# Moving a residual addition from GpSimd to VectorE, with three changes of order, in a fused attention and Mamba kernel

## The chip, the cores and the metric

The kernel runs on one core of one Trainium2 chip. The metric is the device time of one execution in microseconds (us); of several runs the median is given. TensorE is called PE in the profile, VectorE DVE, ScalarE ACT, GpSimd POOL, and SyncE SP; SP here only issues DMAs. "PEld" is the loading of weights into PE.

## The reference, cut to what matters

```python
# x: (8, 512, 48, 48) fp32, that is 8 samples of 512 channels by 2304 tokens
x = x + linear_causal_attention(groupnorm(x))   # 8 heads of 64; q, k = elu + 1; out = num / den
y = groupnorm(x)
prev = None
for i in range(4):                              # four slices of 128 channels
    x_i = y[i] + prev if prev is not None else y[i]
    x_m = mamba_i(x_i)                          # in_proj, conv of 4 taps, silu, x_proj, softplus,
                                                # scan over tokens with 16 states of 256 channels,
                                                # gate by silu(z), out_proj
    f = maximum(x_i, x_m)
    prev = feats[i] = sigmoid(mean(x_i)) * x_i + sigmoid(mean(f)) * f
x = x + concatenate(feats)
```

Everything is fp32.

## The kernel before, in words

Both layers run at once. The work of a sample and a slice of 128 channels is a block, 32 in all, and a block is six chunks of `LC` = 384 tokens. Two streams take the blocks by turns: stream 0 has the even samples, stream 1 the odd ones. The kernel is written out by hand in program order (a manual schedule); each engine works through its own instructions in that order, and waits are made for the data and buffers they need.

**Mamba's scan** is the frame. A chunk of a block is a `Job` (192 in all), and a job is eight slots (`SLOTS`), one for each of two halves of the 256 channels and four quarters of the 16 states. In a slot (`slot`):

- `product` on DVE (L890) and `last_product` on POOL (L879) multiply B with delta times x. POOL does the last `TAIL` columns of each of four groups, DVE the others. DVE reads B from a copy in PSUM (`Bp`), which ACT makes in `inputs` (L863).
- `decay` on ACT (L900) makes exp(A delta) in a PSUM bank, up to three ahead (`DEPTH`), five ahead in two places.
- `scan` on DVE (L910), four of them, each giving its bank back.
- `weigh` on POOL (L923) multiplies by C; `gather` on PE (L937) sums over the states into `yp`.

At the end of each half of a job DVE multiplies by the gate (`gated`, L949), and after the second PE projects (`Job.project`, L955) and DVE takes the maximum (`maximum`, L966). Tiles `u` of a slot go round in five buffers.

**All else is done beside the slots**, in stages. A slot has two halves; `beside` is called in each half, at the slot's start for the even one, behind the second scan for the odd one. Stages are Python generators wrapped in `Task`. At each yield a stage says when it is due (a half number, or a gap since its last step) and how many PSUM banks it needs (six are shared with the decays; `take` gives the first free one). `tasks` holds the Mamba stages and `heads` the attention's chunks (`chunk`). `beside` first steps the heads that need no bank, and then goes through tasks and heads in this order, so what a task issues in a half stands ahead of a head's stages that need banks:

```python
for t in heads:
    if t.need is not None and t.need[1] == 0 and t.fits() and t.due():
        t.step()
held = False
for t in tasks + heads:
```

The parts of these stages that the change touches:

- `chunk`, counted in halves from the chunk's own start (`at(j)`); chunks follow each other by 16 halves, the length of a job. At 0, 2 and 4 PE projects q, k and v (`project`, L300) and ACT and DVE make the features (L312, L313, L359, L367); L373 and L375 are the running sum of k, which ACT copies (L382) and DVE multiplies with q (L386). At 14 and 15 the denominators' reciprocals (`rd`, L433, L434) are spread over 64 columns by ACT (`rdb`, L441). At 17 PE transposes them into a bank (L445, three transposes; one bank needed). At 18 DVE multiplies q by them (L450). At 19 PE makes the masked scores in two banks (L457, L467), at 20 ACT takes their relu out (`sm`, L479) and gives the banks back, and at 22 PE reads the relus (L498). ACT copies the result (L508), and DVE takes its statistics at 28 (L512).
- `pass_on`, run at the end of each block for each of the next block's chunks c. `first` is the half at which that chunk's job begins. At first - 33 three loads go to SP's queue (`loads`: `xb`, `fu`, `xo`; L620, L623, L625), at first - 25 PE mixes two products in a bank (L678), in the next half ACT copies the mixture to `fu` (L682) and PE adds a third (L684), and in the one after that ACT makes the next block's input (L689) and POOL adds `fu` to the residual `xo` (L696). `save` puts the store to `out` on a list; `flush` issues it two halves later.
- `prepare`, for each job: the convolution on PE (L722) from first - 21, four Silus on ACT at first - 18 (L758 to L763), Softplus some halves later (L793). Exp, Silu and Softplus each need ACT's table loaded anew. `dx` is made on POOL (L834); B, C, `dr` and `dxr` are read by DMA (L812, L819, L825).
- `statistics` takes the first group norm's statistics of later samples piece by piece (L253), and `group_norm` its small arithmetic (L190 to L211).
- In the first of a sample's four attention passes POOL also normalises the input, four instructions a chunk (L324).

Of the kernel before, what the change touches and what calls it, by code (L numbers as in the profile page):

```python
# [12 lines left out]
ALU = mybir.AluOpType  # L13
# [6 lines left out]
LC = 384  # L20
NI, NQ, NGR = 4, 4, 4
SLOTS = 8
TAIL = 152
BANKS = 6
DEPTH = 3
LEAD = 11
# [23 lines left out]
def attention_then_mamba_kernel(  # L50
# [12 lines left out]
    nc = tc.nc  # L63
# [106 lines left out]
    def save(out, in_):  # L170
        stores.append((half_no[0], out, in_))

    def flush(every=True):
        while stores and (every or stores[0][0] <= half_no[0] - 2):
            _, o, i = stores.pop(0)
            nc.sync.dma_start(out=o, in_=i)
# [103 lines left out]
    def chunk(m):  # L280
# [10 lines left out]
        def at(j, gap=1):  # L291
            return times[m] + j, gap
# [146 lines left out]
        yield at(15), 0  # L439
        rdb = new("rdb", 1, (P, 2 * NT, 64))  # L440
        nc.scalar.copy(rdb, rd.unsqueeze(2).to_broadcast([P, 2 * NT, 64]))  # L441
        yield at(17), 1
        rb = bank()[:, 0:LC].rearrange("p (i t) -> p i t", i=NT)
        for i in range(NT):
            nc.tensor.transpose(  # L445
# [19 lines left out]
        for i in range(NT):  # L465
            for h, sc in zip(heads_of, scs):
# [5 lines left out]
                    stop=i == NT - 1,  # L472
                    skip_group_check=True,
                )
        yield at(20), 0
        sms = []
        for par, sc in enumerate(scs):
            sm = new(f"sm{par}", 1, (P, NT, T))
# [43 lines left out]
    class Stream:  # L522
# [55 lines left out]
        def pass_on(self):  # L578
# [9 lines left out]
            last = old is not None and old[1] == 3 and not self.samples  # L588
# [26 lines left out]
            def loads(c):  # L615
                fu = xb = xa = None
                cols = slice(c * LC, (c + 1) * LC)
                if not last:
                    xb = mpool.tile([P, LC], F32, tag="xb", name=f"xb_{self.n}_{c}")
                    nc.sync.dma_start(out=xb, in_=x1s[self.b][s * P : (s + 1) * P, cols])  # L620
                if old is not None:
                    fu = mpool.tile([P, LC], F32, tag="fu", name=f"fu_{old[2]}_{c}")
                    nc.sync.dma_start(out=fu, in_=old[3][:, cols])  # L623
                    xa = mpool.tile([P, LC], F32, tag="xo", name=f"xo_{old[2]}_{c}")
                    nc.sync.dma_start(out=xa, in_=x1s[old[0]][old[1] * P : (old[1] + 1) * P, cols])  # L625
                return fu, xb, xa

            if last and self.z:
# [5 lines left out]
                for c in range(NC):  # L634
                    fu, xa = (got[c // 2][:, c % 2 * 2 + i, 0:LC] for i in range(2))
# [4 lines left out]
                for c in range(NC):  # L640
                    fu, xa = (got[c // 2][:, c % 2 * 2 + i, 0:LC] for i in range(2))
# [15 lines left out]
            for c in range(NC):  # L657

                cols, icols = slice(c * LC, (c + 1) * LC), slice(3 + c * LC, 3 + (c + 1) * LC)
                if now is None:  # L660
                    first = 2 * self.jobs[self.block * NC + c].start
                    yield (first - 33, 1), 0
                    now = loads(c)
                    yield (first - 25, 1), 0 if old is None else 1
                else:
                    yield "1", 0 if old is None else 1
                fu, xb, xa = now
                now = None
                if not last:
                    normed = dict(bias=norm[:, 1, :], scale=norm[:, 0, :])  # L670
                if old is None:
                    nc.scalar.activation(xi[:, icols], xb, AF.Identity, **normed)
                else:
                    bank = Banks()
                    mixed = bank()[:, 0:LC]
                    more = len(factors) == 3
                    for i, src in enumerate((xi[:, icols], fu)):
                        nc.tensor.matmul(  # L678
                            mixed, mix[:, i, :], src, start=i == 0, stop=i == 1, skip_group_check=True
                        )  # L680
                    yield "1", 0
                    nc.scalar.copy(fu, mixed)  # L682
                    if more:
                        nc.tensor.matmul(  # L684
                            mixed, mix[:, 2, :], xb, start=False, stop=True, skip_group_check=True
                        )
                    yield "1", 0
                    if more:
                        nc.scalar.activation(  # L689
                            xi[:, icols], mixed, AF.Identity, bias=norm[:, 1, :]  # L690
                        )
                    elif not last:
                        nc.scalar.activation(xi[:, icols], xb, AF.Identity, **normed)
                    bank.free()
                    self.ready = c + 1
                    nc.gpsimd.tensor_tensor(xa, xa, fu, ALU.add)  # L696
                    save(out[old[0], old[1] * P : (old[1] + 1) * P, cols], xa)
                self.ready = c + 1
                if last and c + 1 < NC:
                    yield "3", 0  # L700
                    now = loads(c + 1)

    class Job:
# [156 lines left out]
        def inputs(self, pair):  # L860

            self.Bp = psx.tile([P, 2, LC - TAIL], F32, tag="Bp", name=f"Bp_{self.n}_{pair}")
            nc.scalar.copy(self.Bp, self.B[pair % 2][:, :, 0 : LC - TAIL])  # L863

# [7 lines left out]
        def last_product(self, s):  # L872

            shape, cols = [P, NGR, TAIL], slice(LC - TAIL, LC)
            h, q = s // NQ, s % NQ
            u = mpool.tile([P, NGR, 1 + LC], F32, tag="u", name=f"u_{self.n}_{s}", bufs=5)
            if self.c:
                nc.scalar.copy(u[:, :, 0], self.state[:, h, q, :])  # L878
            nc.gpsimd.tensor_tensor(  # L879
                u[:, :, 1 + LC - TAIL :],  # L880
                self.B[q // 2][:, q % 2, cols].unsqueeze(1).to_broadcast(shape),
# [5 lines left out]
        def product(self, s, u):  # L887

            shape, cols = [P, NGR, LC - TAIL], slice(0, LC - TAIL)
            nc.vector.tensor_mul(  # L890
                u[:, :, 1 : 1 + LC - TAIL],
                self.Bp[:, s % 2, :].unsqueeze(1).to_broadcast(shape),
# [100 lines left out]
    class Task:  # L993
# [16 lines left out]
        def due(self):  # L1010
# [4 lines left out]
                return half_no[0] >= when  # L1015
            return half_no[0] - self.last >= int(when[0])

        def finish(self):
            while self.need is not None:
                self.step()  # L1020
# [27 lines left out]
    for b in counted:  # L1048
        first = times[parts.index((b, 0, 0))]
        begins[b] = (first - 20) // PERIOD * PERIOD - 4 * NC * PERIOD - 2 if b > 1 else first - 64  # L1050

    def begin(latest):

        nonlocal begun, put
        while counted and begins[counted[0]] - 4 <= half_no[0]:
            tasks.append(Task(statistics(counted.pop(0))))
        while put < len(parts) and times[put] - 6 <= half_no[0]:
            put += 1
            heads.append(Task(chunk(put - 1), before=heads[-1] if heads else None))
        while (  # L1060
            begun < len(jobs)
            and jobs[begun].start <= latest
            and jobs[begun].stream.block == jobs[begun].block
            and jobs[begun].stream.ready > jobs[begun].c
        ):
            tasks.append(Task(jobs[begun].prepare(), jobs[begun].start))
            begun += 1

    def prune():
        tasks[:] = [t for t in tasks if t.need is not None]  # L1070
        heads[:] = [t for t in heads if t.need is not None]

    def beside(half):

        half_no[0] = half
        flush(every=False)
        begin(half // 2 + LEAD)

        for t in heads:
            if t.need is not None and t.need[1] == 0 and t.fits() and t.due():  # L1080
                t.step()
        held = False
        for t in tasks + heads:
            while t.need is not None and t.due():
                if not t.fits() or held and t.need[1]:
                    held = held or t.need[1] > len(spare)
                    break
                t.step()
        prune()
# [19 lines left out]
    def at(k):  # L1109
        return jobs[k // SLOTS], k % SLOTS  # L1110
# [43 lines left out]
    def slot(k):  # L1154
# [9 lines left out]
        elif s == 6:  # L1164
            job.gated(0)
        beside(2 * k)
        for i in range(4):
            job.scan(s, i, us[k], decays.pop(0))
# [40 lines left out]
    with tc.manual_schedule():  # L1209
        half_no[0] = FIRST - 6  # L1210
        Task(statistics(0)).finish()
        load_scales()
        for st in streams:
            tasks.append(Task(st.weights()))
            tasks.append(Task(st.pass_on()))
        for half in range(FIRST - 6, 0):
            beside(half)
        prime(0)
        for k in range(slots):
            slot(k)  # L1220
# [88 lines left out]
```

## Time and profile before

| what | value |
|---|---|
| median of 3 runs | 8270.86 us (8269.19 to 8271.96) |
| the profiled execution | 8283.94 us, its span 8282.2 us |
| granted TensorE clock in it, mean | 0.944 |
| busy: DVE, POOL, PE, ACT | 7829.1, 7753.9, 7354.5, 6991.8 us |
| DMA engines' mean share | 76.6% |
| L696, the addition on POOL | 186 x 1010 ns |
| L450, the product of q with the reciprocals, on DVE | 192 x 547 ns, 143.2 us of waits for L445 |
| waits of PE at L678 for ACT's L479 | 241.4 us, 173 times |

A group of instructions is named by its line, its engine and its operation; the two numbers behind the bar are its busy time in all and the mean time of one instruction in ns, and then come the idle time of the engine just before them and what ended most of it. A recorded duration overlaps the next instruction on its engine by some 0.05 to 0.1 us, so that the sum of a group's durations is somewhat above what it occupies. In the lists of waits the columns are total us, how many times, and the longest. In timelines they are start, us from first start to last end, instruction, and in brackets the idle time ahead and what ended it.

### The profile page before, as it was taken

The page shows a single profiled execution, that of the slowest core. Times are in us where ns is not written, and L with a number is a line of the kernel's source. Part 1 is how long each engine was busy: PE and PEld are TensorE (multiplying, and loading weights), DVE is VectorE, ACT ScalarE, POOL GpSimd, SP SyncE. Part 2 cuts the span into 40 slices and gives each one's busy share as a digit, 9 for nine tenths or more (in the row PEclk, how much of TensorE's full clock was granted, in tenths as well). Part 3 has the DMA queues.
Part 4 walks back from the last instruction along what each step waited for, and adds up shares of the span by engine and source line. Part 5 has one row for each costly group of instructions (what it writes and reads, how often), then busy time and mean ns, then how long its engine had stood idle before and what let it go on. Part 6 is the DMA issues. An engine that isn't in the chain of part 4 may idle for free. (4 is left out here: it accounts for less than half of the span.)

```text
span 8282.2 us, 133009 instructions
## 1 busy us (share of the span) xinstructions
PE 7354.5 (89%) x39882; PEld 3572.9 (43%) x39882; DVE 7829.1 (95%) x10534; ACT 6991.8 (84%) x14914; POOL 7753.9 (94%) x3905
## 2 busy tenths in 40 slices
PE   8889999998889999998889999999988999998975
PEld 4444444444444444444444444444444444444421
DVE  3999999999999999999999999999999999999998
ACT  3888888888888888888888888888888888888876
POOL 2999999999999999999999999999999999999998
PEclk9999999999999999999999999999999999999976
DMA  6777778777777788777787777877777777777765
GB/s 201 189 189 206 206 200 210 205 196 205 206 200 201 199 210 209 203 205 197 204 213 201 199 206 203 210 207 197 209 204 203 203 201 195 200 200 195 191 170 146
DMA packets 1097348, 1654.99 MB, mean 200 GB/s; under 512 B 143913, under 2 KB 989353, under 8 KB 1096498
## 3 DMA queue, kind: packets, MB, share of 16 engines
q1 hardware_dynamic: 1096626, 1646.48, 76.6%
q8 instruction: 316, 5.18, 0.3%
q14 instruction: 406, 3.33, 0.1%
HBM read 1318.23 MB, written 327.68 MB: 199 GB/s over the span
## 5 line engine op out<-in xcount | busy, mean ns | idle before, releaser
L910 DVE TENSOR_TENSOR_SCAN u<-bank,u 128x385 f32<-128x385 f32 (+1 forms) x6144 | 5447.2, 939 | 115.2 <-ACT bank L900 112.9
L923 POOL TENSOR_TENSOR u<-u,C 128x1536 f32<-128x1536 f32 x1536 | 4894.5, 3187 | 349.1 <-DVE u L910 210.3
L900 ACT ACTIVATE bank<-dr,scales 128x385 f32<-128x385 f32 (+1 forms) x6144 | 3414.1, 579 | 612.8 <-DVE u L910 574.6
L879 POOL TENSOR_TENSOR u<-B,dxr 128x608 f32<-128x608 f32 x1536 | 2286.1, 1488 | 14.5 <-DMA x<-xr 13.8
L300 PE MATMUL bank<-xn,wq 128*128 128x384 f32 x4608 | 1886.5, 558 | 286.1 <-DVE u L910 233.4
L890 DVE TENSOR_TENSOR u<-Bp,dxr 128x928 f32<-128x928 f32 x1536 | 1690.2, 1100 | 10.9 <-ACT Bp L863 7.2
L937 PE MATMUL yp<-u,cst 128*32 128x384 f32 x12288 | 1353.7, 513 | 200.8 <-POOL u L923 122.8
L300 PEld LDWEIGHTS bank<-xn,wq 128*128 128x128 f32 x4608 | 955.4, 216 | 1189.5 <-DVE u L910 373.4
L722 PE MATMUL bank<-xi,wk 128*128 128x384 f32 x3072 | 1102.4, 502 | 7.6 <-ACT xr L508 7.0
L722 PEld LDWEIGHTS bank<-xi,wk 128*128 128x128 f32 x3072 | 555.9, 191 | 561.4 <-DVE u L910 107.7
L937 PEld LDWEIGHTS yp<-u,cst 128*32 128x32 f32 x12288 | 249.1, 109 | 776.7 <-issue 415.7
L900 ACT ACT_TABLE_LOAD x382 | 490.1, 1283 | 6.8
L312 ACT ACTIVATE ex<-bank,bqkv_sb 128x384 f32<-128x384 f32 x384 | 221.4, 577 | 311.5 <-PE bank L300 311.4
L863 ACT COPY Bp<-B 128x464 f32<-128x464 f32 x768 | 420.5, 548 | 21.3 <-DVE u L890 13.1
L834 POOL TENSOR_TENSOR dx<-delta,xs 128x384 f32<-128x384 f32 x384 | 386.0, 1005 | 21.5 <-ACT delta L793 21.5
L678 PE MATMUL bank<-xi,mix 128*128 128x384 f32 x372 | 175.4, 554 | 249.6 <-ACT sm L479 241.4
L955 PE MATMUL bank<-yz,scales 128*128 128x384 f32 x768 | 329.1, 541 | 51.3 <-DVE yz L949 41.7
L782 PE MATMUL bank<-dbc,steps_w 9*128 9x384 f32 x768 | 306.4, 519 | 22.3 <-DVE rd L433 17.6
L733 PE MATMUL bank<-xi,scales 128*128 128x384 f32 x768 | 296.3, 496 | 18.9 <-ACT xs L758 18.8
L769 PE MATMUL bank<-xs,scales 128*40 128x384 f32 x768 | 285.0, 494 | 0.0
L498 PE MATMUL bank<-sm,v 128*64 128x128 f32 x2304 | 254.7, 299 | 0.0
L878 ACT COPY u<-state 128x4 f32<-128x4 f32 x1280 | 249.2, 195 | 0.0
(123 smaller groups left out, 8193.6 us busy)
## 6 DMA issues: line engine op xcount, KB each, us to landing
dr<-dscr SPq DMA_DIRECT2D x1536, 192.0 KB, 4.7
dxr<-xscr SPq DMA_DIRECT2D x1536, 192.0 KB, 5.3
xn<-xn SPq DMA_DIRECT2D x192, 768.0 KB, 5.1
B<-scr SPq DMA_DIRECT2D x1536, 96.0 KB, 4.2
C<-scr SPq DMA_DIRECT2D x1536, 96.0 KB, 2.6
dscr<-delta SPq DMA_DIRECT2D x192, 384.0 KB, 4.8
xscr<-dx SPq DMA_DIRECT2D x192, 384.0 KB, 2.9
xn<-in_x SPq DMA_DIRECT2D x48, 768.0 KB, 5.1
```

The lines of the kernel that those rows point to most:

```text
L300: nc.tensor.matmul(ps, wqs[m // NC][:, kt, j * P : (j + 1) * P], xn[:, kt, :], start=(kt == 0), stop=(kt == 3),)
L722: nc.tensor.matmul(xc, wk[:, k, h * P : (h + 1) * P], xi[:, c0 + k : c0 + k + LC], start=(k == 0), stop=(k == 3),)
L782: nc.tensor.matmul(vp, steps_w[32:41, s, h * P : (h + 1) * P], dbc[32:41, :], start=True, stop=True)
L834: nc.gpsimd.tensor_tensor(dx[:, h, :], delta[:, h, :], xs[:, h, :], ALU.mult)
L863: nc.scalar.copy(self.Bp, self.B[pair % 2][:, :, 0 : LC - TAIL])
L879: nc.gpsimd.tensor_tensor(u[:, :, 1 + LC - TAIL :], self.B[q // 2][:, q % 2, cols].unsqueeze(1).to_broadcast(shape), self.dxr[h][:, :, col ...
L890: nc.vector.tensor_mul(u[:, :, 1 : 1 + LC - TAIL], self.Bp[:, s % 2, :].unsqueeze(1).to_broadcast(shape), self.dxr[s // NQ][:, :, cols],)
L900: nc.scalar.activation(dA[:, cols], self.dr[h][:, g, cols], AF.Exp, scale=w_a[:, self.w[1], NGR * h + g, q : q + 1],)
L910: nc.vector.tensor_tensor_scan(u[:, g, cols], dA[:, cols], u[:, g, cols], 0.0, ALU.mult, ALU.add,)
L923: nc.gpsimd.tensor_tensor(u[:, :, 0:LC], u[:, :, 1:], self.C[q // 2][:, q % 2, :].unsqueeze(1).to_broadcast([P, NGR, LC]), ALU.mult,)
L937: nc.tensor.matmul(self.yp[g * 32 : g * 32 + 32, 0:LC], state_sum, u[:, g, 0:LC], start=False, stop=s % NQ == NQ - 1, skip_group_check=True,)
L955: nc.tensor.matmul(self.xm[:, 0:LC], w_out[:, self.w[1], h, :], self.yz[:, h, :], start=(h == 0), stop=(h == 1),)
```

## The change

Four edits. The addition to the residual goes from POOL to DVE, and from the half of the block input's making to a stage of its own at first - 17, the half behind that of the job's Silus; in the last pass of a stream it comes one half later. The loads move from first - 33 to first - 30. A head's stage may now carry a word: "first" puts it into the early round of `beside` though it needs a bank (the transposes of L445), "late" keeps it out of that round though it needs none (the relus of L479). `TAIL` goes from 152 to 160 columns.

```diff
-TAIL = 152
+TAIL = 160
...
-        yield at(17), 1
+        yield at(17), 1, "first"
         rb = bank()[:, 0:LC].rearrange("p (i t) -> p i t", i=NT)
...
-        yield at(20), 0
+        yield at(20), 0, "late"
         sms = []
...
                     first = 2 * self.jobs[self.block * NC + c].start
-                    yield (first - 33, 1), 0
+                    yield (first - 30, 1), 0
                     now = loads(c)
...
                     bank.free()
                     self.ready = c + 1
-                    nc.gpsimd.tensor_tensor(xa, xa, fu, ALU.add)
+                    yield (first - 17, 1) if not last else "1", 0, "late"
+                    nc.vector.tensor_add(xa, xa, fu)
                     save(out[old[0], old[1] * P : (old[1] + 1) * P, cols], xa)
...
+        def early(self):
+            return self.need[2] == "first" if len(self.need) > 2 else self.need[1] == 0
+
...
         for t in heads:
-            if t.need is not None and t.need[1] == 0 and t.fits() and t.due():
+            if t.need is not None and t.early() and t.fits() and t.due():
                 t.step()
```

In the changed file the addition stands on L697, and lines from there on are numbered one higher up to `Task`, four higher behind it.

## The prediction

> **What bounds the kernel now.** I read the page's busy times first, then the groups of VectorE (DVE) and GpSimd (POOL) with their shapes, then the waits of DVE, and last the timeline of one job in the middle of the run. A job is one chunk of 384 tokens of a Mamba block: eight slots, 192 jobs in all.
>
> The page, parts 1 and 5:
>
> ```profile
> PE 7354.5 (89%) x39882; PEld 3572.9 (43%) x39882; DVE 7829.1 (95%) x10534; ACT 6991.8 (84%) x14914; POOL 7753.9 (94%) x3905
> ...
> L910 DVE TENSOR_TENSOR_SCAN u<-bank,u 128x385 f32<-128x385 f32 (+1 forms) x6144 | 5447.2, 939 | 115.2 <-ACT bank L900 112.9
> L923 POOL TENSOR_TENSOR u<-u,C 128x1536 f32<-128x1536 f32 x1536 | 4894.5, 3187 | 349.1 <-DVE u L910 210.3
> ...
> L879 POOL TENSOR_TENSOR u<-B,dxr 128x608 f32<-128x608 f32 x1536 | 2286.1, 1488 | 14.5 <-DMA x<-xr 13.8
> ...
> L890 DVE TENSOR_TENSOR u<-Bp,dxr 128x928 f32<-128x928 f32 x1536 | 1690.2, 1100 | 10.9 <-ACT Bp L863 7.2
> ```
>
> Two engines are nearly full. DVE's idle time is 453 us, 137 of it in the first 200 us (windows of 200 us), so DVE sets the pace and what is left to win beside its own work is some 300 us. POOL's 528 us is the next limit. The waits of DVE, with total us, times and longest:
>
> ```profile
> DVE q L450 <- PE bank L445: 143.2, 129, 4.2
> DVE u L910 <- ACT bank L900: 112.9, 137, 4.8
> DVE pr L386 <- ACT before L382: 30.9, 66, 4.2
> ```
>
> The first is one attention product that waits for three transposes. The second lies nearly all behind the Silu slot, where ScalarE (ACT) loads two tables of 1.28 us each and the scans run out of decays. The timeline of that slot, DVE then POOL:
>
> ```profile
> 2725.00 0.55 DVE L512 BATCH_NORM_STATS2 stats_m<-xr 128x6 f32<-128x384 f32 x1
> 2725.47 0.94 DVE L910 TENSOR_TENSOR_SCAN u<-bank,u 128x385 f32<-128x385 f32 x1
> 2727.39 2.65 DVE L910 TENSOR_TENSOR_SCAN u<-bank,u 128x385 f32<-128x385 f32 x3 [0.98 <-ACT bank L900]
> ```
>
> ```profile
> 2725.39 1.49 POOL L879 TENSOR_TENSOR u<-B,dxr 128x608 f32<-128x608 f32 x1
> 2728.49 3.18 POOL L923 TENSOR_TENSOR u<-u,C 128x1536 f32<-128x1536 f32 x1 [1.61 <-DVE u L910]
> ```
>
> DVE stalls 0.98 us, and POOL, which has caught up, waits 1.61 us for the slot's last scan. The moved addition lands in DVE's queue just behind the L512 at 2725.00.
>
> [...] Every large two-input DVE operation of this kernel reads PSUM on one side, but the group norm's small ones (L198, L199) do not:
>
> ```profile
> 1699.68 3.18 DVE L198 TENSOR_TENSOR gm_a<-gm_a 128x4 f32<-128x4 f32 x1
> 1702.89 1.39 DVE L199 TENSOR_TENSOR gm_a<-gm_a,mv_a 128x4 f32<-128x4 f32 x1
> ```
>
> ```profile
> 1699.68 3.17 POOL L923 TENSOR_TENSOR u<-u,C 128x1536 f32<-128x1536 f32 x1 [2.15 <-DVE gm_a L191]
> 1702.79 1.47 POOL L879 TENSOR_TENSOR u<-B,dxr 128x608 f32<-128x608 f32 x1
> ```
>
> Four elements take 3.18 and 1.39 us, ending with POOL's instruction; without POOL beside them they take 0.16. So L198 slipped in between L923 and L879. It does not always: at 1960.18 one took 3.63 us, past three such borders. The new addition has both inputs in SBUF. [...] the 384-wide rows here take 549 (L386), and the next instruction starts 0.46 to 0.47 us after one begins. I use 0.46.
>
> **The change part by part**, in us of the whole run.
>
> *TAIL 152 to 160.* DVE's product goes from 928 to 896 elements. Slope from the rows L890 and L386: (1100-549)/(928-384) = 1.01 ns, so 32 x 1.01 x 1536 = -50 on DVE. POOL's grows from 608 to 640: (3187-1488)/(1536-608) = 1.83 ns, 59 ns each, +90 on POOL. ACT's copy to PSUM (L863) shrinks by some 14 ns x 768 = 11, hidden by its 575 us of waits for banks.
>
> *Addition to DVE.* POOL loses L696, 186 x 1.01 = -188; net POOL -98. POOL's relief counts only where it sets the pace: the first pass of each later pair of samples (around 1800 to 2300, 3800 to 4300 and 5800 to 6300 us, 36 jobs), where L324 is added and its idle time is 0.7 to 1.8 us a job. DVE gains 186 x 0.46 = +86. Of this the Silu stall hides min(stall, 0.46) in each job; summed over the trace's jobs that have an addition, 53 of their 88 us of stall (it is 0 where two statistics L253 already fill the place, 0.87 where none does). Net +33.
>
> *The port.* At the place of the addition L879 is usually running, with 0.8 to 1.5 us to go. Afterwards POOL gets there 0.97-7x0.06 = 0.55 earlier, but DVE also comes earlier by what the next item saves (about 0.7 a job), so I keep 0.5 to 0.8 us: 93 to 150. The rest of the Silu stall (88-53 = 35) hides some: +58 to +115, middle +87. Behind the waiting addition stand the last two scans of the slot; POOL's next weighing (L923) waits for them, and PE's gather (L937) for that. [...]
>
> *Transposes first.* The instruction order on PE changes by L445 standing ahead of the two-matmul product L955 instead of behind, and by nothing else. L450 then comes as early as L955's 1.6 us; but the next but one on DVE, L966, needs L955, so a stall longer than L450 and L359 (2 x 0.46 = 0.92) returns there. Sum of min(stall, 0.92) over jobs 12 on: -86 of 129. Worse than 0 would need L966 to be late otherwise; it has 0.9 us of cover.
>
> *Relu behind the fused products.* PE now stands 241 us in front of L678 for the bank that the relu (L479) gives back. In the new order L678 takes the bank that L367 on DVE frees, about 0.75 us sooner; the value projection (L300) waits for L479 in its place. PE spends the gain waiting for DVE's banks later (L300 <- DVE u L910, 233 us), so I count only the small stalls of L386 and L949 in the steady part, -15 of 24. The relus' readers (L498) come two halves later, 5 us, which covers them.
>
> *Loads at first - 30.* Three DMAs (xb, fu, xo) on SP's queue pass behind four dxr reads, four dr reads and the scr store; out's store moves behind dxr. L678 needs them five halves (13 us) later, and they land in 2.5 to 4.3. Each dxr read is issued 1.4 us earlier; DVE waited for dxr 2.7 us in all. Nothing either way.
>
> Sum: -50 +33 +87 -86 -15 = **-31**. Against the profiled execution's 8283.94 that is 8253; the median of the runs, 8270.86, is 0.16% below that execution, and gives 8240.
>
> **Rivals.** (1) *The addition slips in at once*, or POOL is idle by then: the port item goes, -118, of which POOL's pace in the 36 jobs takes back some 15: 8168. For it: L198 got in behind L923 in all three cases where L879 followed; the jobs whose DVE is early would meet that border. Against: in most jobs shown L879 has already begun. (2) *The port closes a loop between DVE and POOL*, slower. In the job shown POOL runs from 2728.49 to the next L879's end in 39.5 us without a gap; afterwards 39.5-0.96+8x0.06 = 39.0. If the addition must await that end, then 0.46 and two scans (1.71) follow before POOL may go on: 41.2 a job at least, and the job takes 41.0 now, so steady jobs win nothing. In the 36 jobs with L324 POOL never waits now; there each loses the 2.2 us: 36 x 2.2 = +79, so -31+79 = +48, 8319. It decides if the addition fails to get in before POOL's queue runs dry. For it: the L198 of 3.63 us, and L593's 2.8 to 5.3 us. (3) *The order moves do nothing* because L445 still waits for the projection L300 before it: -31+86 = +55 at worst, but TAIL and the hidden part stay, and DVE is then later at the port, which saves about as much: 8271, no change.
>
> **How the numbers follow.** A measurement of this kernel can tell about 0.2%, 16.5 us, from no change. Forecast (8211 to 8268 by the port item's ends): 0.45; rival 1: 0.22; rival 2: 0.28; rival 3: 0.05. Faster: 0.36 of the forecast's part and rival 1, 0.58. Same: 0.08 of the forecast and rival 3, 0.13. Slower: rival 2 and a corner of the forecast, 0.29. The forecast's own range is 8211 to 8268; for 8 in 10 it reaches to both rivals, 8160 to 8325.
>
> **What would show it.** In the profile after: DVE's row for the addition (now L697) has a mean of 1.0 to 1.4 us, not 0.55; L450's wait falls below 50 us and some 20 to 40 appears at L966; L890 is near 1068 ns and L879 near 1547; POOL's wait at L923 for DVE grows. A mean of 0.6 says rival 1, one of 2 or more with DVE late in the L324 stretches says rival 2, L450 still near 140 says rival 3. The forecast is wrong if the sum of the addition's excess over 0.46 us is not what separates the time from -118.

## The result, and the profile after

The changed kernel takes 8333.92 us (median of 4 runs, 8330.55 to 8339.77) against 8271.41 us before: a ratio of 1.0076, 95% interval 1.0058 to 1.0093. It is 62 us slower where 31 us faster was forecast. The profiled execution took 8330.55 us, its span 8328.6.

The page after, parts 1 and 5 (lines stand one higher than before, from L697 on):

```profile
PE 7571.1 (91%) x39882; PEld 3603.7 (43%) x39882; DVE 8091.0 (97%) x10720; ACT 6990.1 (84%) x14914; POOL 7690.2 (92%) x3719
...
L911 DVE TENSOR_TENSOR_SCAN u<-bank,u 128x385 f32<-128x385 f32 (+1 forms) x6144 | 5421.4, 934 | 18.3 <-ACT bank L901 18.1
L924 POOL TENSOR_TENSOR u<-u,C 128x1536 f32<-128x1536 f32 x1536 | 4890.4, 3184 | 444.3 <-DVE u L911 338.2
...
L880 POOL TENSOR_TENSOR u<-B,dxr 128x640 f32<-128x640 f32 x1536 | 2392.1, 1557 | 30.0 <-DMA x<-xr 14.5
...
L891 DVE TENSOR_TENSOR u<-Bp,dxr 128x896 f32<-128x896 f32 x1536 | 1632.1, 1063 | 14.2 <-ACT Bp L864 7.2
...
L697 DVE TENSOR_TENSOR xo<-xo,fu 128x384 f32<-128x384 f32 x186 | 348.7, 1875 | 0.0
```

The last row is the result. The addition has a mean of 1875 ns, where other 384-wide operations of VectorE take 527 to 553, and no idle time stands ahead of it: the wait is inside the recorded duration, so that VectorE looks busier (8091 us against 7829) and is not more useful. It is a wait for GpSimd: 184 of the 186 additions end 0.40 to 0.47 us behind the end of a GpSimd instruction. The product is 37 ns shorter, as intended, and the two largest waits fell (columns: total us, times, longest):

```profile
DVE q L450 <- PE bank L445: 25.7, 35, 5.8
DVE u L911 <- ACT bank L901: 18.1, 18, 2.9
```

They were 143.2 and 112.9. VectorE's idle time went from 453 to 238 us, and its busy time went up by 262: 261.9 - 215.4 = 46.5, the 46 us by which the span grew. The timeline of one steady job, VectorE then GpSimd:

```profile
6678.85 0.55 DVE L512 BATCH_NORM_STATS2 stats_m<-xr 128x6 f32<-128x384 f32 x1
6679.32 2.28 DVE L697 TENSOR_TENSOR xo<-xo,fu 128x384 f32<-128x384 f32 x1
6681.52 2.65 DVE L911 TENSOR_TENSOR_SCAN u<-bank,u 128x385 f32<-128x385 f32 x3
```

```profile
6642.08 3.16 POOL L924 TENSOR_TENSOR u<-u,C 128x1536 f32<-128x1536 f32 x1 [2.28 <-DVE u L911]
...
6676.49 3.20 POOL L924 TENSOR_TENSOR u<-u,C 128x1536 f32<-128x1536 f32 x1
6679.63 1.55 POOL L880 TENSOR_TENSOR u<-B,dxr 128x640 f32<-128x640 f32 x1
6683.46 3.16 POOL L924 TENSOR_TENSOR u<-u,C 128x1536 f32<-128x1536 f32 x1 [2.28 <-DVE u L911]
```

The addition starts at 6679.32, while GpSimd is in L924. It does not get in when L924 ends (6679.69), waits through L880 to 6681.18, and is done at 6681.60. Two scans of the slot follow (the third in that line belongs to the next slot), and only then may GpSimd begin the next weighing, after 2.28 us of idling. That closes a loop: from 6642.08 to 6681.18 GpSimd works 39.1 us without a gap, then the addition and two scans cost 2.28 us in which it can do nothing, and this job takes 41.38 us. As long as VectorE reaches the addition before that L880 ends, what it saved earlier in the job does not shorten it.

### The profile page after: what moved, and what is told of

Same layout as the page of the kernel before. It is cut to its first block, busy times and chain, and to the rows that moved or that the text cites. A ratio compares the mean times of both kernels' runs of the same rounds, so it can differ in the third digit from the quotient of the medians.

```text
span 8328.6 us, 133118 instructions
## 1 busy us (share of the span) xinstructions
PE 7571.1 (91%) x39882; PEld 3603.7 (43%) x39882; DVE 8091.0 (97%) x10720; ACT 6990.1 (84%) x14914; POOL 7690.2 (92%) x3719
## 5 line engine op out<-in xcount | busy, mean ns | idle before, releaser
L924 POOL TENSOR_TENSOR u<-u,C 128x1536 f32<-128x1536 f32 x1536 | 4890.4, 3184 | 444.3 <-DVE u L911 338.2
L880 POOL TENSOR_TENSOR u<-B,dxr 128x640 f32<-128x640 f32 x1536 | 2392.1, 1557 | 30.0 <-DMA x<-xr 14.5
L300 PE MATMUL bank<-xn,wq 128*128 128x384 f32 x4608 | 1962.8, 577 | 189.7 <-DVE u L911 162.6
L891 DVE TENSOR_TENSOR u<-Bp,dxr 128x896 f32<-128x896 f32 x1536 | 1632.1, 1063 | 14.2 <-ACT Bp L864 7.2
L938 PE MATMUL yp<-u,cst 128*32 128x384 f32 x12288 | 1415.7, 534 | 192.1 <-POOL u L924 143.8
L300 PEld LDWEIGHTS bank<-xn,wq 128*128 128x128 f32 x4608 | 994.6, 225 | 1173.0 <-DVE u L911 346.0
L783 PE MATMUL bank<-dbc,steps_w 9*128 9x384 f32 x768 | 369.2, 601 | 108.8 <-DVE u L911 86.8
L864 ACT COPY Bp<-B 128x448 f32<-128x448 f32 x768 | 409.5, 533 | 34.8 <-DMA B<-scr 24.8
L697 DVE TENSOR_TENSOR xo<-xo,fu 128x384 f32<-128x384 f32 x186 | 348.7, 1875 | 0.0
L783 PEld LDWEIGHTS bank<-dbc,steps_w 9*128 9x128 f32 x768 | 136.0, 208 | 330.6 <-ACT bank L901 177.9
```

What stands on the lines that cost most here:

```text
L300: nc.tensor.matmul(ps, wqs[m // NC][:, kt, j * P : (j + 1) * P], xn[:, kt, :], start=(kt == 0), stop=(kt == 3),)
L697: nc.vector.tensor_add(xa, xa, fu)
L783: nc.tensor.matmul(vp, steps_w[32:41, s, h * P : (h + 1) * P], dbc[32:41, :], start=True, stop=True)
L880: nc.gpsimd.tensor_tensor(u[:, :, 1 + LC - TAIL :], self.B[q // 2][:, q % 2, cols].unsqueeze(1).to_broadcast(shape), self.dxr[h][:, :, col ...
L891: nc.vector.tensor_mul(u[:, :, 1 : 1 + LC - TAIL], self.Bp[:, s % 2, :].unsqueeze(1).to_broadcast(shape), self.dxr[s // NQ][:, :, cols],)
L924: nc.gpsimd.tensor_tensor(u[:, :, 0:LC], u[:, :, 1:], self.C[q // 2][:, q % 2, :].unsqueeze(1).to_broadcast([P, NGR, LC]), ALU.mult,)
```

## The experiments

Theory P: the addition, with two inputs in SBUF, waits for GpSimd's instructions. "Port" in the prediction and in the expectations is the author's name for this wait; what in the chip stands behind it was not shown. Rivals: the lower TensorE clock (0.916 against 0.944) and the order moves make it slow (C); the long L697 only renames the wait for ACT that stood there (W). Each median stands against 8272 to 8275 us of the kernel before, measured beside it; intervals are of the ratio to it.

**The addition back on GpSimd, at its new place** (e1_add_on_pool).

```diff
-                    nc.vector.tensor_add(xa, xa, fu)
+                    nc.gpsimd.tensor_tensor(xa, xa, fu, ALU.add)
```

> The changed kernel with the addition of L697 on GpSimd again, at its new place. Theory P (the port: the addition's two SBUF inputs wait for GpSimd, 186 x (1.87-0.47) = 260 us of DVE time): without it the order moves and TAIL show alone. DVE is relieved of 349 us of L697; the Silu stall comes back (about 95 us), GpSimd gets 188 us more and becomes the pace in part: 8140 to 8230 us, below the kernel before. Rival C (the lower TensorE clock, 0.916 against 0.944, and the order moves make it slow): 8300 us or more, clock still near 0.92. Rival W (L697's length only renames the wait for ACT that stood there): 8250 to 8290.

Measured: 8195.47 us, ratio 0.9907 (0.9892 to 0.9922), clock 0.938. All of the change but the engine of one addition makes the kernel 77 us faster; that engine costs 138 us at `TAIL` 160. C and W fall.

**One SBUF input at the same place** (e2_one_input). The addition to the output is left out.

```diff
-                    nc.vector.tensor_add(xa, xa, fu)
+                    side = small.tile([P, 6], F32, tag="side", name=f"side_{old[2]}_{c}")
+                    nc.vector.bn_stats(side, xa)
```

> The changed kernel with the addition replaced by a bn_stats of xo (384 columns, one SBUF input) into a small tile at the same place on VectorE; the output's addition is left out. Theory P: the instruction takes 0.55 us as all other bn_stats do, 250 us of waiting for the port go, of which some 60 come back as the wait for ACT behind the Silus: 8110 to 8190 us. Rival C: 8300 us or more, since order, engine, place and TAIL are the same. Rival W: within 30 us of the changed kernel, with about 200 us of wait at the scans instead.

Measured: 8163.86 us, ratio 0.9871 (0.9856 to 0.9885). The group that stands in for L697, and the wait for decays that returned:

```profile
L698 DVE BATCH_NORM_STATS2 side<-xo 128x6 f32<-128x384 f32 x186 | 100.2, 539 | 0.0
```

```profile
DVE u L912 <- ACT bank L902: 58.3, 99, 3.3
```

Same engine, place and order, 248 us less in the row (348.7 to 100.2), and the kernel is 170 us faster. Of the other 78 us, 67 came back as waits: 40 at the scans, 15 at L450, 12 at L968. So this instruction, which reads SBUF once, does not wait (all 186 take 531 to 551 ns), and the wait costs 170 us net. By itself the run does not say that it is the second input, since the stand-in also writes 6 columns instead of 384; the next run writes all 384. What the 100 us of the stand-in itself cost is not shown either: no run leaves the place empty on both engines.

**The addition reading PSUM** (e3_add_from_psum), in place of ACT's copy of the mixture.

```diff
-                    nc.scalar.copy(fu, mixed)
+                    nc.vector.tensor_add(xa, xa, mixed)
...
-                    yield (first - 17, 1) if not last else "1", 0, "late"
-                    nc.vector.tensor_add(xa, xa, fu)
```

> The changed kernel, but the addition reads the mixed product from its PSUM bank (one input in SBUF, one in PSUM), in the place of ACT's copy to fu, which goes (186 x 0.48 us of ACT). Theory P: 0.55 us each, no port wait; 86 us on DVE of which nothing is hidden behind the Silus, the Silu stall comes back: 8130 to 8220 us. Against it: VectorE can now wait for the products of L678 (ACT waited 59 us there), up to 1 us each: 8290 at worst. Rival C: 8300 us or more.

Measured: 8203.44 us, ratio 0.9918 (0.9903 to 0.9933). The addition itself, still on VectorE and with one input in SBUF and one in PSUM:

```profile
L682 DVE TENSOR_TENSOR xo<-xo,bank 128x384 f32<-128x384 f32 x186 | 100.6, 541 | 2.2 <-PE bank L678 2.2
```

541 ns and 2.2 us of waiting for PE; all 186 take 527 to 555 ns, while GpSimd is 94% busy. That is P once more, with the same arithmetic and the same 384 columns written, though at another place. Of what the run before changed it is then the second SBUF input that counts (1875 ns with two, 541 with one). The kernel is no faster than with the addition on GpSimd (8195, intervals overlap). That no Silu stall hides the addition here (110 us of waits for decays are back) fits this, but was not tried apart.

**The move alone** (e4_move_alone): the kernel before with the addition's move and the loads at first - 30; TAIL, transposes and relus as before.

> The kernel before with the addition on VectorE in its new place and the loads at first - 30 alone; TAIL 152, transposes and relus where they were. Theory P: the addition again takes 1.3 to 2 us; the gains of TAIL (58 us) and of the transposes (117 us of L450's wait) are missing, though part of that wait is covered by VectorE being late: 8380 to 8460 us. Rival C or W: at most 8310 us.

Measured: 8373.69 us, ratio 1.0124 (1.0107 to 1.014), 6 us below the range. L450 waits 168 us, and the addition waits less than in the changed kernel:

```profile
L697 DVE TENSOR_TENSOR xo<-xo,fu 128x384 f32<-128x384 f32 x186 | 208.4, 1121 | 0.0
```

The next run has the same `TAIL` 152 and the two order moves besides, so it parts the way from here to the changed kernel in two.

**TAIL 152 in the changed kernel** (e7_tail152), which tells a loop from a fixed price.

> The changed kernel with TAIL back at 152. Theory L (the port closes a loop: GpSimd's work of a job, then the addition, then two scans; the job's length is set by GpSimd's work): GpSimd has 8 x 0.06 = 0.5 us less a job, VectorE 0.27 us more: the port wait falls, and the time stays or falls: 8270 to 8335 us. Theory B (VectorE is simply full and each addition costs a fixed 1.4 us more): 50 us slower than the changed kernel, 8370 to 8395 us, the addition still near 1.87 us.

Measured: 8282.2 us (20 runs, 8272.3 to 8290.15), ratio 1.001 (1.0004 to 1.0017): 52 us faster than with 160, though VectorE's product is 8 columns a group longer. The row:

```profile
L697 DVE TENSOR_TENSOR xo<-xo,fu 128x384 f32<-128x384 f32 x186 | 267.0, 1436 | 0.0
```

From e4_move_alone to this run, by the order moves, VectorE's wait at L450 falls by 142 us (168 to 26), L697's row grows by 59, and the kernel is 91 us faster. From here to the changed kernel, by 8 columns, the product's row falls by 48.5 us, L697's row grows by 82, and the kernel is 52 us slower. So what VectorE saves elsewhere comes back in this wait in part where only VectorE saved, and more than in full where GpSimd also got longer. The columns by themselves do not do it: with the addition on GpSimd, 160 and 152 take 8195 and 8182 us (e1_add_on_pool and e9_pool_tail152), and the intervals overlap.

The traces give, for jobs 102 to 107, GpSimd's time from the weighing of a job's last slot to the end of the last L880 before the next such weighing, and its gap after that: 39.24 + 2.31 = 41.55 us in the changed kernel, 38.78 + 2.30 = 41.08 here. The gap is the same, and the job is shorter by the 0.46 us that GpSimd's work is shorter. In these jobs this is the loop; a fixed price for each addition would have given 50 us the other way. It is not closed everywhere: from one addition to the next, GpSimd's only idle time over 0.1 us is the one at the addition in 83 of 185 cases in the changed kernel, in 71 here and in 21 with the move alone.

**Transposes first, alone** (e5_first_alone), and **with the relus late** (e8_first_and_late), both on the kernel before.

```diff
-        yield at(17), 1
+        yield at(17), 1, "first"
```

> The kernel before with the transposes of L445 put first in their half, and nothing else. The step of the prediction: L450's wait of 143 us falls by min(stall, 0.92) per job, 86 us, and 20 to 30 us of it appear at L966: 8185 to 8215 us. Rival (VectorE only gets on to the next wait, for GpSimd or ACT): 8245 to 8272 us, with L450's wait gone all the same.

Measured: 8204.61 us, ratio 0.9914 (0.9898 to 0.9931). Two of VectorE's waits:

```profile
DVE q L450 <- PE bank L445: 30.9, 35, 4.2
DVE fg L966 <- PE bank L955: 17.2, 17, 2.2
```

112 us go from L450, 15 appear at L966, a little less than expected, and 68 us are gained, within the range.

```diff
-        yield at(20), 0
+        yield at(20), 0, "late"
```

> The kernel before with the transposes first and the relus late; TAIL 152, addition on GpSimd in its old place, loads at first - 33. Against e5_first_alone it shows the relus' part: predicted 0 to -15 us (the wait of L386 gone, PE's wait at L678 for the relu of 241 us gone). Rival: PE is at 90% and short of time, so that 2 us a job of PE's time is worth 50 us or more.

Measured: 8171.62 us, ratio 0.9872 (0.9857 to 0.9886), another 33 us: more than the 15 expected, less than the rival's 50. PE's wait for the relu at L678, 241 us in the kernel before and 158 with the transposes alone, is gone, and in its place stands

```profile
PE bank L678 <- DVE k L367: 31.7, 70, 1.2
```

and VectorE's waits at L386 and L949 fall from 32.8 and 21.6 us with the transposes alone to 15.2 and 7.2, by 32 us together, about what was gained (its idle time in all fell by 30.5).

**Columns and places without the wait** (e6_psum_tail176, e10_psum_tail152, e9_pool_tail152, e11_first_late_tail144). The next four are sizes of the above.

> The addition reading PSUM (as in e3_add_from_psum) with TAIL 176. VectorE's product has 64 columns less than at 160: 64 x 1.03 ns x 1536 = 101 us off VectorE, 64 x 1.8 x 1536 = 177 us more on GpSimd, which waited 268 us for scans at TAIL 160. If VectorE sets the pace: 8100 to 8150 us. If GpSimd does (it was 94% busy): 8210 to 8290 us, its wait for scans under 120 us.

Measured: 8213.73 us, ratio 0.9921 (0.9906 to 0.9935); GpSimd's wait for scans is 118 us. Both are what was expected if GpSimd sets the pace, but the interval overlaps that of `TAIL` 160.

> The addition reading PSUM with TAIL 152. e6_psum_tail176 was 10 us above TAIL 160, so neither engine alone sets the pace; GpSimd has 188 us less than with the addition, so fewer columns for it should be worse here: 8215 to 8250 us. If GpSimd's place in the loop counts and not its sum: 8160 to 8200 us.

Measured: 8212.59 us, ratio 0.9928 (0.9911 to 0.9945). It lies just under the first range and above the second. With 152, 160 and 176 columns the kernel that reads PSUM takes 8213, 8203 and 8214 us, which cannot be told apart.

> The changed kernel with the addition on GpSimd at its new place and TAIL 152: all of the change but the move to VectorE and the 8 columns. Against e8_first_and_late (8172) it shows the place of the addition and the loads; against e1_add_on_pool (8195) the columns. If GpSimd sets part of the pace with the addition on it, TAIL 160 costs there (90 us of GpSimd for 58 of VectorE): 8140 to 8175 us. If VectorE alone sets it: 8215 to 8245 us.

Measured: 8182.49 us, ratio 0.9892 (0.9877 to 0.9907). In neither range. Its interval overlaps those of e1_add_on_pool and e8_first_and_late, so neither the 8 columns nor the new place on GpSimd can be told from nothing.

> The kernel before with the transposes first and the relus late, and TAIL 144. VectorE has 8 x 1.03 ns x 4 x 1536 = 51 us more, GpSimd 90 us less. VectorE sets the pace: 8190 to 8222 us; GpSimd: 8110 to 8160 us.

Measured: 8160.24 us, ratio 0.9863 (0.9848 to 0.9878). It lies at the edge of GpSimd's range, but 8 columns fewer are worth nothing that can be told (8172 at 152, intervals overlap). This and e8_first_and_late are the fastest kernels that still make the whole output: the two order moves, with the addition left on GpSimd in its old place.

## Why the prediction was wrong, point by point

- **What bounds the kernel**: VectorE, with GpSimd next: right, but taken as two separate limits. With the addition waiting for GpSimd they became one loop (41.55 us a job in jobs 102 to 107).
- **The wait for GpSimd** (the item "port"), the step that failed. That the addition would wait was right. Its size was not: 0.5 to 0.8 us each, +58 to +115 us after what the Silu stall hides. The recorded mean is 1.87 us, 1.33 above the 0.54 of the addition that reads PSUM, or 248 us over 186 additions, and 170 net by the run with one input. The prediction let GpSimd reach the place 0.55 us sooner and VectorE 0.7 sooner, called that a draw, and kept the wait seen in the trace of before. The runs show no draw: the same excess is 0.58 us with the move alone, inside the range, 0.90 with the order moves, and 1.33 with the 8 columns too. Where the loop is closed GpSimd cannot start sooner than the last job's scans let it, so that a VectorE that comes sooner waits longer. The prediction's own test, that the excess over 0.46 us separates the time from -118, gives 263 us where 180 were measured; the long wait also covers other waits, of which 67 us came back with one input.
- **The sum** added the wait and `TAIL` as if one did not touch the other. With `TAIL` 152 it holds: -101 us for the order moves (-101 forecast) and +111 for the addition and its loads (e7_tail152 against e8_first_and_late; +33 and +87 forecast). Then 8 columns more cost 52 where -50 was forecast. Seen from the other side, with `TAIL` 160 and one input the kernel is 108 us faster than before, close to the -118 forecast without the wait, and then the wait costs 170 instead of 87. Either way nearly all of the error of 93 us lies where the two items meet.
- **Rival 2** was this loop: 39.0 us of GpSimd, then 0.46 and two scans, 41.2 us a job at least. The trace has 39.24 + 2.31 = 41.55 in the jobs measured. That its time, 8319 us, came close to 8334 is in part luck: the sum -31 + 79 kept the gain of the steady jobs, which its own "steady jobs win nothing" rules out, and put the loss in the stretches with L324 alone. Of the 46 us between the two profiled executions 28 lie in the later jobs with L324 and 20 in the other jobs from 12 on (the start gained 1). A job takes 44.04 us against 42.92 in jobs 90 to 95, which have L324, and 41.55 against 41.33 in jobs 102 to 107. Its sign came in those stretches only: the addition's mean there is 2.5 to 2.6 us, and 1.4 to 2.1 elsewhere. That a blocked addition is passed over at a border, the point at which rival 2 decides, is what happens mostly behind L924 (last section).
- **Transposes**: -86 predicted, -68 measured, with the wait returning at L966 as said. Right.
- **Relus**: -15 predicted, -33 measured, by the waits named (L386 and L949). Right in its mechanism; the two waits fell by 32 us, where 15 of 24 in the steady part had been counted.
- **TAIL**: -50 predicted from VectorE's slope. The product did shrink by 37 ns, 58 us in all. But in the changed kernel the 8 columns cost 52 us, with GpSimd the loop's long side, and where no addition waits for GpSimd they show nothing either way (three pairs of runs, all with intervals that overlap).
- **Loads at first - 30**: priced at nothing; no run parts them from the addition's place, and e9_pool_tail152 against e8_first_and_late bounds both together within the intervals.
- **Addition hidden by the Silu stall**: 53 us predicted. The wait for decays is 117.6 us with the addition on GpSimd (e1_add_on_pool) and 58.3 with the one-input instruction in its place, 59 less: right. ACT's table loads, two of which stand in that stall, take 1.28 us each: in the trace of before 192 at the Silus (L758), 192 at the Softplus (L793) and 382 at the decays behind the two (L900).
- **A reading**: not every large two-input operation of VectorE read PSUM before; the twelve of L644, behind 8270 us, read SBUF twice. Nothing in the forecast rests on them.

## What to carry to other kernels

Before work goes from GpSimd to VectorE, look at where its inputs lie: with two in SBUF the addition here still ran behind GpSimd, and the profile books the wait as busy time (1875 ns in the mean, 0.0 us of idle ahead), so compare its mean with that of a like instruction that reads PSUM (541 ns). If the waiting instruction stands in front of what GpSimd waits for next, write out the loop of both engines and take its length as a likely time, not only as a rival. More work for GpSimd is then more time (8 columns, 52 us), and part of what VectorE saves elsewhere goes into a longer wait (59 of 142 us). Try the parts of a change apart, and together: here two moves of order were worth 101 us, or 91 with the addition on VectorE; that addition cost 111, and 8 columns, which showed nothing without it, cost another 52 on top.

## What the runs showed of the hardware that was not expected

When GpSimd had a next instruction ready, an addition that waited for it mostly did not get in between. Of 94 additions of the changed kernel that began beside an L924, 25 got in when it ended and 69 were passed over; beside L880, after which GpSimd has to wait for the scans in 83 of 90 cases, all 90 got in when it ended. So a wait up to the end of the running instruction, which the prediction's 0.5 to 0.8 us took, is only the shortest one. One of each at the border of L924 and L880, VectorE then GpSimd:

```profile
3400.04 0.73 DVE L697 TENSOR_TENSOR xo<-xo,fu 128x384 f32<-128x384 f32 x1
...
3825.67 2.28 DVE L697 TENSOR_TENSOR xo<-xo,fu 128x384 f32<-128x384 f32 x1
```

```profile
3400.31 1.86 POOL L880 TENSOR_TENSOR u<-B,dxr 128x640 f32<-128x640 f32 x1
...
3826.01 1.53 POOL L880 TENSOR_TENSOR u<-B,dxr 128x640 f32<-128x640 f32 x1
```

In the first GpSimd's L880 is 0.33 us longer, as it would be if it then waited for VectorE (1.87 us in the mean where an addition got in, 1.55 where it was passed over); in the second it passes. The two began 0.32 and 0.37 us before L924's end, and what decides was not found.

One SBUF input was no guarantee. L593 adds 1 to two columns of one tile in SBUF, and its shortest takes 0.17 us; its mean in the kernel before is 0.88:

```profile
L593 DVE TENSOR_SCALAR wt<-wt 128x2 f32<-128x2 f32 x32 | 28.2, 883 | 0.3 <-ACT wt L591 0.3
```

Six of the 32 take 2.8 to 5.3 us, and 31 end 0.02 to 0.03 us behind the end of a GpSimd instruction, before and after the change, which looks like the same wait. The one-input statistics at the place of L697 never showed this (539 ns in the mean). Which one-input instructions wait was not tried.

The last thing is TensorE's granted clock: 0.916 in the changed kernel and 0.926 in it with TAIL 152, against 0.934 to 0.946 in the others. No run shows that it cost time: VectorE's waits for PE are small in both (25.7 and 26.2 us at L450), and the slowest kernel of all, the move alone, has 0.934. Its cause was not tried.
